# 3x3 convolutions by transformed tiles: from tiles of four by two pixels to tiles of four by four, with the products on column halves of the array

## The chip, the cores and the metric

The kernel runs on one core of a Trainium2 chip. The metric is device time in microseconds (us). Before the change two runs took 2594.91 and 2595.62 us, with a median of 2595.26 us. Engines have short names below: PE is TensorE (PEld its weight loads), DVE is VectorE, ACT is ScalarE, POOL is GpSimd, and SP is the engine that starts most transfers.

## The reference, cut to what matters

The input x is (8, 512, 32, 32) in float32: eight images of 512 channels. The program is two residual layers, and the first one holds the convolutions that are changed.

```python
cbs = silu(bn(conv2d(x, w)))                 # w is 1x1 or 3x3
t = cbs(gn(x), cv1_w)                        # 1x1, 512 -> 512
ys = [t[:, :256], t[:, 256:]]
for i in range(2):
    z = cbs(ys[-1], m_cv1_w[i], pad=1)       # 3x3, 256 -> 256
    z = bot_attention(z, m_qkv_w[i], ...)    # 4 heads, 1024 positions
    ys.append(ys[-1] + cbs(z, m_cv2_w[i]))   # 1x1, 256 -> 256
y = x + cbs(concat(ys), cv2_w)               # 1x1, 1024 -> 512
out = y + L1(gn(y))                          # depthwise 3x3, prune, 1x1, prune
```

So there are 2 x 8 = 16 convolutions of 3x3 in all, called l=0 and l=1 of each batch.

## The kernel before, in words

**Order of the work.** The eight batches are unrolled one after the other. Every piece of work is a small function that is registered under a short name with `add` (line 307). Four strings, FIRST (45), HEAD (64), TAIL (80) and LAST (87), list these names in the order in which the pieces are issued, and `go` (310) issues them. The wrapper `InOrder` (95) keeps that order on each engine, so no scheduler moves anything. Batch 0 runs FIRST; every later batch runs HEAD and then TAIL or LAST. HEAD holds the new batch's 1x1 convolution `cv1`, its first 3x3 convolution, attention and second 3x3 convolution, and beside them what remains of the previous batch's second layer: the depthwise taps `t` on DVE (594) and the pointwise products.

**One convolution** (`conv3`, 725). The input lies in `yp`, split by column phase: pixel column 4t + r is stored under r, so a tile of four columns is read without strides. An output tile is four pixels wide and two high; 6 x 4 = 24 products for each of 128 tiles replace the nine taps. The pieces are:
- `d`: `along_rows` (746) makes `vtmp` and `v`, `across_rows` (774) makes the operands in `kr`, `vt` and `qy`, one for each j = 0, 1, 2. All of this is on DVE, but for four border strips on ACT.
- `P`: `products` (791), six pieces (j by output half m) of 16 matmuls of 128x128 weights by 128 columns. Each takes one tile of 1.05 MB from the weight ring.
- `Rc` and `R`: `rows_back` (810). ACT copies a quarter of the product bank ps_c to `c`; DVE adds the rest from the bank, four instructions of 256 elements.
- `B` and `E`: `along_back` (833) and `ends` (853), on DVE. `Ez`: `close` (858), the silu on ACT that makes half m of `z`.

**Around it.** `c`/`ca` and `y`/`ya` are the halves of `cv1` with their activations (684); `k`, `ka`/`kd`, `v`/`va` and `q`/`qa` are the key, value and query products (`qkv`, 890) into the banks ps_qk and ps_v, which need `z`; `m`, `ma`, `mr` are the 1x1 convolution after the attention (`cv2m`, 1077), with `mr` the residual that writes the next `yp`. The last convolution of batches 1 to 6 (`quartered`, 1243) leaves partial sums `kept` from the banks ps_q on DVE, which run beside the second 3x3 convolution.

**Weights.** In batch 0 `transform_weights` (322) makes the 24 transformed planes of each layer's weights on DVE and ACT and stores them in device memory (`store`, 349), six tiles of 1.05 MB for each layer. From then on every convolution loads them through a ring of five buffers (`ring_sources` 388, `ring_load` 413), which also carries the other large weights. Work tiles share a pool of 11 buffers; the product banks are two pairs of PSUM banks (`big_tile`, 162).

The engines' instructions all appear under L105 in the profile, the line of the wrapper, so groups are told apart by their tiles.

Of the kernel before, what the change touches and what calls it, by code (L numbers as in the profile page):

```python
# [27 lines left out]
PITCH = F // 4 + 1  # L28
# [17 lines left out]
    g*6 gm gd gv g gp g gb gm gd ga gv ga c gp fo gb c ta0 ga ta0 ga ta0 ti0 fo ta2 to0*2 c  # L46
    ti0*2 ca ta2*2 c rl ca ta1*3 ti2 ti1 to1 d ti1 d y ya to1 ti1 y ya ti2 to2 d y ti2 d to2 rl
    ya y d*2 ya d P Rc R P d*3 Rc R d*2 P Rc R B P Rc R B*2 P*2 Rc R E Ez B Rc R E Ez k*2 X k dw
    ta0 ka k kp ka ta0*2 v kp ti0 v va ti0 v ti0 q v va ta1 q ta1 qa q*2 qa ta1 s e s e p to0 s
    e p w to0 s e w*2 ti1 s e p ti1*2 p s e p w s to1 s e p w e p w s w to1 ta2 e s e w h p z  # L50
    ta2 s e p ta2 s ti2 e w*2 s e w ti2 to2 ti2 s e w s e to2 w s e w s e w s e rh p w p*5 h z
    s*2 w e*2 n s e w p s p w nr e p w nr*2 s e nc s nr e ns p w s e p w*2 nc s e p w h z s e s
    w s*2 p*2 e w p e*2 p sc p w sc s w e p w s e p w*3 h z n nr*4 ns nc sc Q K m ma sc dp mr
    m*2 ma mr m ma mr ma mr d*4 Q nc K d*3 P d P Rc R d*2 Rc R d*2 P Rc R P*2 Rc B R B P Rc R E
    Ez Rc B*2 R E Ez k X dx k*3 ka*2 kp*2 v*2 q v*2 va*2 cw*3 rk cw q*2 qa q qa s*2 e*2 p s e p
    w s e w s p cw*2 e s e w s e p rk p w s e p*2 s e w s e g*2 w*2 p w h z s e w cw s e p*2
    cw*2 rk s e w*2 s e w s*2 p e rk w p s e g w p g p s*2 e g w g e*2 p w h z p s w e g p w n
    nr s e nr p w g s e s p w nr e s e w p w*2 s nr p e s e w h ns p s e p nc*2 s w e p w s e p
    w s e p w s sc e p s e p w sc w*3 h z n nr*2 Q nr*2 ns z Q sc*2 nc m*2 ma mr ma mr m ma nc m
    ma mr gm mr gd Q gv u A Q x u i A x i gp i*2 Q gb ga*4 Q im id Q iv A Q x ip i*2 ib b bm t*3  # L60
    Q A t x i*2
# [3 lines left out]
    t c*2 t b im id bm c ca iv t ip t l t*2 ib lr b t*3 c bm ca b y d y bm d ya d*2 ya d*3 y P d  # L65
    Rc R d*2 P Rc R d ya P d Rc R B P Rc R P B*2 Rc R E P Ez Rc B R E Ez y k*3 ya k ka X lp ka
    kd*2 t*5 v*2 l t va v*2 va t lr q*2 t*2 lp t q qa s q e qa s e p s t e w t s e w l s*2 p*2 w
    e*2 p w s p e s w t s w t e s e p lr e p w*2 h z s e p w s t w s p s e p e*2 w*2 p s e w s t
    e p s w p s e w e t p*2 w lp t h z s*2 e*2 w s*2 n e p*2 e w*2 s nr s p e w nr e p s e w nr
    s nr t p ns l w e p*2 w lr lp w ot h s e s w p ot w s w s e*2 p*2 e w p s e w s e ot p*2 z  # L70
    sc w nc w*2 h n nc o O nr ok Ok z nr*2 sc nr ns o ou oa O*2 Ou sc Oa m sc nc m*2 ma*2 m ma
    mr ot mr ma mr o nc mr ou d Ou o O d ou Ou o d O ou*2 oa Ou*2 d Oa o O P d*2 Rc d*3 R P d*2
    Rc R d P Rc P R B Rc P B Rc P R B*2 Rc R ou E oa Ou R Oa o O dp E Ez*2 X k v k v ou oa Ou
    fr*2 Oa ka kd f*2 fr*2 f*2 dx va k v*2 k va q*4 ka kd qa*2 s*3 e*2 p e w p s e w s*2 e*2 p*3
    w s*2 g e*2 w*2 s p e w*2 s e w p s*2 h g e g p w s w z p e*2 s w e g*2 s*2 w*2 p e*2 g p*3
    g s w*2 e p s e w h s*2 e*2 p z p w*2 s p e p s n nr*3 w e s g e p w p s w*3 e p s nc e nr s
    ns e nc w s h s p w z w e p s e w s p e*2 p sc s w e p*2 w s sc e p w*3 h n nr*4 ns z
# [3 lines left out]
    Q*2 K r2 nc r0 Q r2 sc Q m r0 sc K m*2 ma nc mr ma m r0*2 ma mr r1*2 mr Q*3 ma mr r2 r1*2 u0  # L81
    r2 a0 u1 gm a1 gd Q x1 u0 r3 gv x0 gp r3*2 u0 Q r3 gb u0*2 Q u0 a0 i a0 ga Q i x0*2 ga Q i
    u0 a0 i im id ga Q iv ip u1 x0 Q u1*2 ib u1 b a1 x1 bm Q ga u1 t a1 i t Q x1 u1 i*2 a1 t i t
    x1
# [3 lines left out]
    Q sc nc*2 m ma m sc m*2 ma rg ma mr*2 ma mr*2 Q*2 A x Q i*2 im id rg iv ip ib b bm Q*2 t A x  # L88
    i*2 Q im id t*3 iv ip t ib t Q t b Q bm t Q*2 t A t l lr x i*2 im t lp id t iv ip t A ib t b
    bm Q t A x t*2 l lr o x i*2 o lp o*2 im t id t o*3 iv ip t*2 o ib b t*3 bm t o*4 t*2 o*4 l t  # L90
    lr lp t*4 l lr lp o*10 oa o*2 oa fr f oa*2 fr f o*3 oa o oa fr oa f oa fr f
# [34 lines left out]
def fast_kernel(  # L126
# [54 lines left out]
    def load(dst, b):  # L181
# [14 lines left out]
    yp = [const_tile([P, 4, 2, F, PITCH], f"yp{l}") for l in range(2)]  # L196
# [9 lines left out]
        [dram.tile([P, 2, 4, 2, P], F32, tag=f"u{l}_{i}", name=f"u{l}") for i in range(6)]  # L206
# [43 lines left out]

    for t in yp:
        nc.gpsimd.memset(t, 0.0)
# [5 lines left out]
    sc12 = const_tile([P, 4], "sc12")  # L258

    def fold_norms():  # L260
# [8 lines left out]
        ab = const_tile([P, 8], "ab")  # L269
        nc.vector.tensor_tensor(ab, v_sb[:, V_AB : V_AB + 8], sc[:, BN4:], ALU.mult)  # L270
        nc.vector.tensor_tensor(bi[:, BN4:], bi[:, BN4:], ab, ALU.add)
        nc.vector.tensor_scalar(sc12, sc[:, BN2 : BN2 + 4], -1.0 / 12.0, None, ALU.mult)
        yield

    dw = v_sb[:, V_DW : V_DW + 9 * KC].rearrange("p (c t) -> p c t", t=9)
# [1599 lines left out]
```

## Time and profile before

| | |
|---|---|
| median of two runs | 2595.26 us |
| span of the profiled execution | 2593.6 us |
| instructions | 36377 |
| PE busy | 2557.7 us (99%) |
| PE weight loads | 1292.0 us (50%) |
| DVE busy | 2054.9 us (79%) |
| ACT busy | 1214.4 us (47%) |
| POOL busy | 129.2 us (5%) |
| moved by DMA | 268.51 MB, 104 GB/s on average |

Times of groups and stages come from the one profiled execution. In a timeline or a list of groups a line gives the engine, the operation, the tile written and the tiles read with partitions x elements, the count, and the idle time before it with what ended it. In a table of windows each engine has its busy time and, in brackets, its number of instructions; the last columns are the granted PE clock as a share of full speed, the share of time that the DMA engines were busy, and GB/s.

### The profile page before, as it was taken

What the parts mean: (1) busy time and instruction counts of PE and PEld (TensorE: products, weight loads), DVE (VectorE), ACT (ScalarE), POOL (GpSimd) and SP (SyncE); (2) the same over time, 40 slices, a digit from 0 to 9 for tenths busy, and PEclk for the clock granted to TensorE, in tenths of its full rate; (3) what the DMA queues carried; (4) which work ended last, traced back from release to release, by engine and by line L of the source; (5) the groups of instructions that cost most, each with busy time, mean ns of one, the idle gap of its engine ahead of it and who ended that gap; (6) DMA issues with size and microseconds to landing.
All of it is one profiled execution on the core that took longest, in us unless ns stands there. A gap on an engine that the chain in (4) does not pass through costs nothing.

```text
span 2593.6 us, 36377 instructions
## 1 busy us (share of the span) xinstructions
PE 2557.7 (99%) x14806; PEld 1292.0 (50%) x14806; DVE 2054.9 (79%) x2954; ACT 1214.4 (47%) x1551; POOL 129.2 (5%) x99
## 2 busy tenths in 40 slices
PE   8999999999999999999999999999999999999997
PEld 5454463634636346463464635545355544645443
DVE  8887588877897877877778778787788877888657
ACT  3635446353463544635445444544445454363534
POOL 1000000000100000000000000000001000010000
PEclk9999999999999999999999999999999999999998
DMA  9445230522305214060140702306122151312300
GB/s 347 157 155 203 66 122 25 167 98 73 113 27 199 66 65 122 17 247 18 65 122 17 248 18 81 105 24 241 33 96 75 61 204 34 130 45 82 122 17 34
DMA packets 83791, 268.51 MB, mean 104 GB/s; under 512 B 7072, under 2 KB 37536, under 8 KB 69408
## 3 DMA queue, kind: packets, MB, share of 16 engines
q1 hardware_dynamic: 76032, 248.01, 27.2%
q0 software_dynamic: 4032, 14.68, 3.1%
q10 hardware_dynamic: 3552, 3.41, 0.4%
q8 instruction: 118, 1.93, 0.3%
q14 instruction: 57, 0.47, 0.1%
HBM read 212.34 MB, written 36.96 MB: 96 GB/s over the span
## 4 chain that ended last, share of the span: by engine, by line
PE 95%; DVE 3%; ACT 1%; issue 0%; DMA 0%; SPq 0%; DVEq 0%; ACTq 0%
PE ps_av L105 16%; PE ps_s L105 16%; PE ps_c L105 13%; PE ps_cv L105 12%; PE ps_qk L105 8%; PE ps_cv2q L105 8%; PE ps_q L105 7%; PE ps_v L105 4%; PE ps_y L105 4%; PE ps_m L105 4%; PE ps_dn L105 1%; ACT qy L105 1%; DVE sum L105 1%; DVE ht L105 1%; PE ps_pw L105 0%
## 5 line engine op out<-in xcount | busy, mean ns | idle before, releaser
L105 ACT ACTIVATE e<-ps_s 128x1024 f32<-128x1024 f32 x512 | 509.7, 1023 | 286.8 <-PE ps_s L105 265.6
L105 PE MATMUL ps_s<-qy,kr 64*64 64x512 f32 x4096 | 513.7, 592 | 1.4
L105 DVE TENSOR_TENSOR sum<-sum,e 128x1024 f32<-128x1024 f32 x384 | 475.2, 1238 | 39.2 <-ACT e L105 19.9
L105 PE MATMUL ps_av<-e,vt 64*64 64x512 f32 x4096 | 506.2, 590 | 0.0
L105 DVE SCALAR_TENSOR_TENSOR ht<-xn,v_sb,ht 128x961 f32<-128x961 f32 (+1 forms) x256 | 317.3, 1247 | 8.6 <-ACT ht L105 5.0
L105 PEld LDWEIGHTS ps_s<-qy,kr 64*64 64x64 f32 x4096 | 160.5, 132 | 289.0 <-issue 191.1
L105 PEld LDWEIGHTS ps_av<-e,vt 64*64 64x64 f32 x4096 | 165.4, 133 | 277.4 <-issue 266.0
L105 PE MATMUL ps_qk<-z,wring 128*128 128x512 f32 x512 | 231.1, 596 | 2.0 <-ACT z L105 1.3
L105 DVE TENSOR_TENSOR sum<-e 128x1024 f32<-128x1024 f32 x64 | 78.1, 1220 | 164.0 <-ACT e L105 162.6
L105 ACT COPY c<-ps_c 128x256 f32<-128x256 f32 x96 | 35.6, 371 | 259.4 <-PE ps_c L105 259.3
L105 PEld LDWEIGHTS ps_qk<-z,wring 128*128 128x128 f32 x512 | 95.6, 190 | 115.7 <-issue 101.5
L105 DVE RECIPROCAL r<-ps_dn 128x128 f32<-128x128 f32 x128 | 113.7, 925 | 11.2 <-PE ps_dn L105 9.0
L105 PE MATMUL ps_c<-vt,wring 128*128 128x128 f32 x1024 | 119.4, 276 | 2.3 <-DVE v L105 1.3
L105 PEld LDWEIGHTS ps_c<-kr,wring 128*128 128x128 f32 x1024 | 116.8, 192 | 8.0 <-issue 6.1
L105 PEld LDWEIGHTS ps_c<-vt,wring 128*128 128x128 f32 x1024 | 116.2, 192 | 4.3 <-ACT c L105 2.3
L105 PE MATMUL ps_c<-qy,wring 128*128 128x128 f32 x1024 | 117.0, 275 | 0.0
L105 PE MATMUL ps_c<-kr,wring 128*128 128x128 f32 x1024 | 117.0, 275 | 0.0
L105 PE MATMUL ps_cv<-pt,w_sb 128*128 128x512 f32 x256 | 116.7, 607 | 0.0
L105 PE MATMUL ps_v<-wring,z 128*128 128x256 f32 x512 | 115.9, 379 | 0.7 <-DVE kr L105 0.7
L105 PEld LDWEIGHTS ps_c<-qy,wring 128*128 128x128 f32 x1024 | 115.6, 192 | 0.0
L105 PE MATMUL ps_m<-z,wm_sb 128*128 128x512 f32 x256 | 112.5, 592 | 0.0
L105 PE MATMUL ps_y<-pt,w_sb 128*128 128x512 f32 x256 | 112.3, 592 | 0.0
(178 smaller groups left out, 3255.5 us busy)
## 6 DMA issues: line engine op xcount, KB each, us to landing
wring<-u SPq DMA_DIRECT2D x96, 1024.0 KB, 4.8
pt<-in_x SPq DMA_DIRECT2D x32, 512.0 KB, 9.4
rw<-r SPq DMA_DIRECT2D x64, 256.0 KB, 3.4
xt<-in_x SPq DMA_DIRECT2D x32, 512.0 KB, 7.5
out<-xt SPq DMA_DIRECT2D x32, 512.0 KB, 8.0
kr<-r POOLq DMA_DIRECT2D x28, 512.0 KB, 6.6
wring<-q SPq DMA_DIRECT2D x14, 896.0 KB, 4.6
wring<-in_wqkv SPq DMA_DIRECT2D x16, 768.0 KB, 4.4
```

The source lines that it names most:

```text
L105: made = method(*args, **kwargs)
```

## The change

The output tiles become four by four: 6 x 6 = 36 products for each of 64 tiles. Pixels in `yp` and in the first layer's tensors are stored by row phase as well as by column phase. The transform along the rows' direction comes first (`by_rows`, into a new buffer `vrows`), then `along_rows` makes the operands for each j. `products` has nine pieces for each convolution instead of six; each goes over four units (m, row), and its 32 matmuls take 128 rows by 64 columns of weights, on the two column halves of the array (o = 0 and 64) in turn, with 64 moving columns. `rows_copy` copies the whole of each product bank (512 and 256 elements) to SBUF on ACT, and `rows_back` works from these copies with small DVE instructions. The weight transform makes four inner rows from three where it made two, and each layer has nine ring tiles instead of six. The activations in `cv1` and `quartered`, the positions and the last residual are cut into two or four instructions, since the phases now nest deeper. The key products are always in the order of z's halves. The four order strings are written anew for these pieces. Of `conv3` only new lines are shown below; those they replace stand in the kernel above.

```diff
...
@@ -25,7 +25,7 @@
 V_BN, V_AB, V_DW, V_RW, V_RH = 0, 96, 104, 140, 268
 V_N = 396
 LIMIT = 1e20
-PITCH = F // 4 + 1
+ROWS = F // 4 * (F // 4 + 1)
 NWORK = 11
 NRING = 5
...
-    yp = [const_tile([P, 4, 2, F, PITCH], f"yp{l}") for l in range(2)]
+    yp = [const_tile([P, 2, 4, 4, ROWS], f"yp{l}") for l in range(2)]
...
     u_dram = [
-        [dram.tile([P, 2, 4, 2, P], F32, tag=f"u{l}_{i}", name=f"u{l}") for i in range(6)]
+        [dram.tile([P, 4, 2, 2, P], F32, tag=f"u{l}_{i}", name=f"u{l}") for i in range(9)]
         for l in range(2)
     ]
...
+    vrows = const_tile([P, 6, 8, HD], "vrows")
...
+    def half_of(l, m, n):
+        if l == 0:
+            t = yp[0][:, m, :, 2 * n : 2 * n + 2, F // 4 :]
+        else:
+            t = yp[1][:, n].rearrange("p q (r k) x -> p q r k x", k=2)[:, :, :, m, F // 4 :]
+        return t.rearrange("p q r x -> p r q x")
...
-                tt(t, planes[j, 0], planes[j, 2], ALU.add)
-            elif step == 1:
+                if step == 0:
+                    tt(t, first, last, ALU.add)
+                else:
+                    stt(t, last, 4.0, first, ALU.mult, ALU.add)
+            elif step in (1, 4):
                 u = work_tile("ucomp")
-                tt(u, box[j], planes[j, 1], ALU.add)
-                store(j, 1, u)
+                if step == 1:
+                    tt(u, box[j], mid, ALU.add)
+                else:
+                    stt(u, mid, 2.0, box[j], ALU.mult, ALU.add)
+                store(j, step // 3 * 2 + 1, u)
             else:
                 t = box.pop(j)
-                tt(t, t, planes.pop((j, 1)), ALU.subtract)
-                store(j, 2, t)
-        def outer_rows(j, c, dy):
+                if step == 2:
...
-                for i in range(6):
+                for i in range(9):
                     yield u_dram[l][i].rearrange("p a b c d -> p (a b c d)"), 2048
...
         def first_end(m):
-            act(inner(yp[0], m - 2), by_phase(flat(open_.pop(m))), AF.Silu, BN0 + m)
+            out = yp[0][:, m - 2, :, :, F // 4 :].rearrange("p q r (i t) -> p r q i t", t=F // 4)
+            src = by_phase(flat(open_.pop(m)))
+            for q in range(4):
+                act(out[:, :, q], src[:, :, q], AF.Silu, BN0 + m)
...
         def half_end(m, n):
-            dst = phases(y0[:, m, :])[:, :, n * 16 : n * 16 + 16]
-            act(dst, by_phase(banks.pop((m, n))), AF.Silu, BN0 + m)
+            dst = phases(y0[:, m, :])[:, :, :, n * 4 : n * 4 + 4]
+            src = by_phase(banks.pop((m, n)))
+            for r in range(4):
+                act(dst[:, r], src[:, r], AF.Silu, BN0 + m)
...
         comps = [t.rearrange("p a b -> p (a b)") for t in (kr, vt, qy)]
...
+        temps, banks, copies = {}, {}, {}
+        slot = {5: 0, 0: 1, 1: 2, 2: 3, 3: 4, 4: 5}
+        slots = vrows if l else vrows.rearrange("p s (r k) x -> p s r k x", k=2)
+        def like(t, o):
+            return t.rearrange("p (g x) -> p g x", x=HD) if len(o.shape) == 3 else t
+        def by_rows(n, step):
+            y = yp[l][:, n]
+            if l == 0:
+                o = [slots[:, slot[k], :, n] for k in range(6)]
+                both = slots[:, :2, :, n]
+            else:
+                o = [flat(vrows[:, slot[k], 4 * n : 4 * n + 4]) for k in range(6)]
+                both = vrows[:, :2, 4 * n : 4 * n + 4]
+            if step == 0:
+                temps["ab"] = work_tile("vtmp")[:, :512]
+                temps["four"] = work_tile("vtmp")
+            ab, four = temps["ab"], temps["four"]
+            own = y[:, :, :, n8:].rearrange("p q g x -> p (q g) x")
+            low, high = own[:, :8], own[:, 8:]
+            a, b = (like(ab[:, i * 256 : (i + 1) * 256], o[0]) for i in range(2))
+            d = [like(four[:, i * 256 : (i + 1) * 256], o[0]) for i in range(4)]
+            parts = four.rearrange("p (s x) -> p s x", s=4)
+            if step == 0:
+                stt(ab.rearrange("p (g x) -> p g x", x=HD), low, -4.0, high, ALU.mult, ALU.add)
+            elif step == 1:
+                tt(o[1], b, a, ALU.add)
+            elif step == 2:
+                tt(o[2], b, a, ALU.subtract)
+            elif step == 3:
+                out = parts[:, 0:4:2].rearrange("p s (g x) -> p s g x", x=HD)
+                tt(out, y[:, 2:, :, n8:], y[:, :2, :, n8:], ALU.subtract)
+            elif step == 4:
+                near, far = (
+                    bass.AP(
+                        y.tensor,
+                        y.offset + at,
+                        [y.ap[0], [4 * ROWS - n8, 2], [ROWS, 4], [1, HD]],
+                    )
+                    for at in (2 * n8, 8 * ROWS + n8)
+                )
+                out = parts[:, 1:4:2].rearrange("p s (g x) -> p s g x", x=HD)
+                tt(out, near, far, ALU.subtract)
+            elif step == 5:
+                stt(o[3], d[0], 2.0, d[2], ALU.mult, ALU.add)
+            elif step == 6:
+                stt(o[4], d[0], -2.0, d[2], ALU.mult, ALU.add)
+            else:
+                i0, i1 = (
+                    i.rearrange("p s (g x) -> p s g x", x=HD) for i in (parts[:, 0:4:3], parts[:, 1:3])
+                )
+                stt(both, i0, -4.0, i1, ALU.mult, ALU.add)
+        n6 = 6 * P
+        zf = z.rearrange("p a b -> p (a b)")[:, : 2 * n6]
+        low, high = (zf.rearrange("p (s r x) -> p r s x", r=2, x=P)[:, i] for i in range(2))
         def along_rows(j, step):
+            p, q = (
+                comps[j][:, i * n6 : (i + 1) * n6].rearrange("p (s x) -> p s x", x=P)
+                for i in range(2)
+            )
+            if step == 0 and j < 2:
+                v = vrows.rearrange("p s (h g) x -> p h s (g x)", h=2)
+                out = zf.rearrange("p (s x) -> p s x", s=6)
+                if j == 0:
+                    stt(out, v[:, 0], -4.0, v[:, 1], ALU.mult, ALU.add)
+                else:
+                    tt(out, v[:, 1], v[:, 0], ALU.subtract)
+            elif step == 0:
+                v = vrows.rearrange("p s (r k) (i t) -> p r s (k i) t", r=4, t=n8)
+                a, b = (t.rearrange("p s (q t) -> p s q t", t=n8) for t in (p, q))
+                e = n8 - 1
+                tt(a[:, :, :, 1:], v[:, 1, :, :, 1:], v[:, 3, :, :, :e], ALU.subtract)
+                nc.scalar.copy(a[:, :, :, 0], v[:, 1, :, :, 0])
+                tt(b[:, :, :, :e], v[:, 0, :, :, 1:], v[:, 2, :, :, :e], ALU.subtract)
+                nc.scalar.mul(b[:, :, :, e], v[:, 2, :, :, e], -1.0)
+            elif j == 0:
+                tt(p if step == 1 else q, high, low, ALU.add if step == 1 else ALU.subtract)
+            elif j == 1:
+                s = 2.0 if step == 1 else -2.0
+                stt(p if step == 1 else q, low, s, high, ALU.mult, ALU.add)
+            elif step == 1:
+                stt(p, p, -4.0, high, ALU.mult, ALU.add)
+            else:
+                stt(q, low, -4.0, q, ALU.mult, ALU.add)
+        place = {1: 0, 3: 1, 2: 2, 4: 3, 0: 4, 5: 5}
+        def products(j, part):
+            u = ring.pop(0).rearrange("p (x i k o) -> p x i k o", x=4, i=2, k=2)
+            for x in range(4):
+                m, row = UNITS[4 * part + x]
+                if (j, m) not in banks:
+                    banks[j, m] = big_tile("ps_c3")
+                ps = flat(banks[j, m])
+                for i in range(2):
+                    at = place[row] * P + i * HD
+                    for k in range(2):
+                        from_ = ((i * 6 + slot[row]) * 2 + k) * HD
+                        for o in (0, HD):
+                            nc.tensor.matmul(
+                                ps[o : o + HD, at : at + HD],
+                                u[:, x, i, k, o : o + HD],
+                                comps[j][:, from_ : from_ + HD],
+                                start=(k == 0),
+                                stop=(k == 1),
+                            )
+            ring_load()
+        inner_planes, outer_planes, ys = {}, {}, {}
+        def rows_copy(j, m, part):
+            if (j, m) not in copies:
+                copies[j, m] = work_tile("c1")
+            c = slice(0, 512) if part == 0 else slice(512, 768)
+            nc.scalar.copy(copies[j, m][:, c], flat(banks[j, m])[:, c])
+        def rows_back(j, m, step):
             if step == 0:
...
+                temps["sd"] = work_tile("c2")
                 if j == 0:
...
+                    inner_planes[m] = work_tile("mid")
+                if j == 2:
+                    outer_planes[m] = copies[j, m]
+            c, sd = copies[j, m], temps["sd"]
+            if step == 0:
+                tt(sd[:, :256], c[:, :256], c[:, 256:512], ALU.add)
+                tt(sd[:, 256:512], c[:, :256], c[:, 256:512], ALU.subtract)
                 return
...
             dst = outer_planes[m][:, :512] if j == 2 else inner_planes[m][:, j * 512 : j * 512 + 512]
...
+            o = dst.rearrange("p (q y x) -> p q y x", q=2, x=HD)
+            s1, s2, d1, d2 = (
+                sd[:, i * P : (i + 1) * P].rearrange("p (q x) -> p q x", x=HD) for i in range(4)
+            )
+            stt(o[:, :, 0], s2, -0.25, s1, ALU.mult, ALU.add)
+            stt(o[:, :, 3], d2, -2.0, d1, ALU.mult, ALU.add)
+            stt(o[:, :, 1], d2, -0.5, d1, ALU.mult, ALU.add)
+            tt(o[:, :, 2], s1, s2, ALU.subtract)
+            e = o[:, :, 0:4:3]
+            outer = c[:, 512:768].rearrange("p (y q x) -> p q y x", y=2, q=2)
+            tt(e, e, outer, ALU.subtract)
...
-        for j in range(3):
-            add("d", *[lambda j=j, i=i: along_rows(j, i) for i in range(2)])
-            add("d", *[lambda j=j, i=i: across_rows(j, i) for i in range(2)])
-        add("P", *[lambda j=j, m=m: products(j, m) for j, m in jm])
-        add("Rc", *[lambda j=j, m=m: rows_back(j, m, 0) for j, m in jm])
-        add("R", *[lambda j=j, m=m: rows_back(j, m, 1) for j, m in jm])
+        add("dr", *[lambda n=n, i=i: by_rows(n, i) for n in range(2) for i in range(8)])
+        add("d", *[lambda j=j, i=i: along_rows(j, i) for j in range(3) for i in range(3)])
+        add("P", *[lambda j=j, i=i: products(j, i) for j in range(3) for i in range(3)])
+        parts = ((0, 0), (0, 1), (1, 1), (1, 0))
+        add("Rc", *[lambda j=j, m=m, i=i: rows_copy(j, m, i) for j in range(3) for m, i in parts])
+        add("R", *[lambda j=j, m=m, i=i: rows_back(j, m, i) for j, m in jm for i in range(2)])
...
         order = [(k, m) for m in (2, 3) for k in range(2)]
-        add("k", *[lambda m=m, k=k: products(m, k) for k, m in (sorted(order) if by_input else order)])
+        add("k", *[lambda m=m, k=k: products(m, k) for k, m in (sorted(order))])
...
         def residual(n, m):
-            r = slice(2 * n, 2 * n + 2)
-            dst = inner(yp[1], m) if l == 0 else phases(qy[:, m, :])
-            nc.vector.tensor_tensor(dst[:, r], phases(ts[n, m]), inner(yp[l], m)[:, r], ALU.add)
+            dst = half_of(1, m, n) if l == 0 else by_rq(qy[:, m, n * 512 : (n + 1) * 512])
+            nc.vector.tensor_tensor(dst, by_rq(ts[n, m]), half_of(l, m, n), ALU.add)
         for name, piece in (("m", products), ("ma", norm), ("mr", residual)):
...
     def to_rows(m, n, t):
-        o = xt[m].rearrange("p (h t r) -> p h t r", t=F // 4, r=4)[:, :, :, 2 * n : 2 * n + 2]
-        i = t.rearrange("p (r h t) -> p h t r", h=F, t=F // 4)
-        nc.vector.tensor_tensor(o, i, o, ALU.add)
+        o = xt[m].rearrange("p (i q t r) -> p i q t r", q=4, t=F // 4, r=4)
+        o = o[..., 2 * n : 2 * n + 2]
+        i = t.rearrange("p (r q i t) -> p i q t r", q=4, i=F // 4, t=F // 4)
+        for r in range(2):
+            nc.vector.tensor_tensor(o[..., r], i[..., r], o[..., r], ALU.add)
     def combine_weights(p):
```

## The prediction

> **What bounds the kernel now.** I read the page first: busy time by engine, the slices, the chain, the costliest groups.
>
> ```profile
> PE 2557.7 (99%) x14806; PEld 1292.0 (50%) x14806; DVE 2054.9 (79%) x2954; ACT 1214.4 (47%) x1551; POOL 129.2 (5%) x99
> ...
> PE   8999999999999999999999999999999999999997
> ...
> DVE  8887588877897877877778778787788877888657
> ...
> PE 95%; DVE 3%; ACT 1%; issue 0%; DMA 0%; SPq 0%; DVEq 0%; ACTq 0%
> ...
> L105 PE MATMUL ps_c<-kr,wring 128*128 128x128 f32 x1024 | 117.0, 275 | 0.0
> ```
>
> TensorE (PE) is never idle and is the chain; the three ps_c groups (the 3x3 products, 3072 records) are 353 us of it. VectorE (DVE) at 79% looks free, but that is a mean. So next the windows of the stages that hold a convolution: first layer (cv1 to qkv), second layer (cv2m to qkv), both of batch 2. Columns: length, then busy of PE, PEld, DVE, ACT, POOL.
>
> ```profile
> 639.15:688.50 49.35, 49.35 (x262) 34.05 (x260) 47.70 (x90) 18.92 (x29) 1.56 (x2) 1.00 0.38 132
> 776.54:820.83 44.29, 44.24 (x246) 31.26 (x244) 39.63 (x79) 12.82 (x27) 0.00 (x0) 1.00 0.36 124
> ```
>
> DVE is at 97% of the first stage. Of the second, its timeline from the last residual to the last correction:
>
> ```profile
> 784.42 0.69 DVE L105 TENSOR_TENSOR yp<-m,yp 128x512 f32<-128x512 f32 x1 [0.97 <-ACT m L105]
> 785.32 0.69 DVE L105 TENSOR_TENSOR kept<-kept,ps_q 128x512 f32<-128x512 f32 x1 [0.21 <-PE ps_q L105]
> ...
> 788.93 1.28 DVE L105 TENSOR_TENSOR kept<-kept,ps_q 128x512 f32<-128x512 f32 x2
> 790.13 1.28 DVE L105 TENSOR_TENSOR kr<-v 128x512 f32<-128x512 f32 x2
> ...
> 810.10 1.09 DVE L105 SCALAR_TENSOR_TENSOR y<-sd 128x256 f32<-128x256 f32 x3
> 811.10 0.41 DVE L105 TENSOR_TENSOR y<-sd 128x256 f32<-128x256 f32 x1
> ...
> 820.18 0.69 DVE L105 TENSOR_TENSOR y<-y,mid 128x512 f32<-128x512 f32 x1
> ```
>
> After 785.32 DVE has no gap to 820.87. ACT then makes the second half of z (ends 822.14 in its timeline), and PE's first values product, which needs all of z, starts at 822.64. DVE is late by half a microsecond of becoming the bound. In the first stage z is complete at 689.51 and its first user could start at 690.2: 0.7 us. So the convolution stages have two bounds, and a change that eases PE and loads DVE is judged by DVE.
>
> **What the skill says.** "TensorEngine Tiling (Array Packing)", Key Properties: different tiles can load weights and multiply in parallel. The trace agrees for 64x64 quadrants: score matmuls start 6 to 7 ns apart in fours, 429 ns per four. Column halves of 64 with all 128 rows do not occur. The same page, Instruction Overhead: about 60 cycles per matmul, so a moving size under that gains nothing; 64 is just above it, and no run shows it. "TensorE: Matmul & The Clock Gate", LDWEIGHTS: the load scales with columns; the trace has 192 ns at 128 columns, 132 at 64, 108 at 32. The same page, Part 1: about 3.4 us of idle halves the PE clock; the trace agrees near the end:
>
> ```profile
> 2566.03 16.82 PE L105 MATMUL ps_pw<-ht,wring 128*128 128x512 f32 x32 [4.74 <-DVE wring L105]
> ```
> ```profile
> 2565.00:2570.00 5.00, 3.98 (x5) 1.85 (x6) 4.86 (x7) 0.00 (x0) 0.00 (x0) 0.50 0.00 0
> ```
>
> A 4.7 us wait, then clock 0.50 (column after POOL).
>
> **PE's part.** Before, a convolution has 96 matmuls of two records; records start 112 ns apart: 96 x 2 x 0.1117 = 21.4 us (about 7.3 for each j in its timeline). After: 288 matmuls of two records, in 144 pairs on two halves, moving size 64. If halves run together, a pair takes for each of its two passes half of 112 plus a few ns, 58: 144 x 2 x 0.058 = 16.7 us, say 16.8. Saving 4.6 us, 16 times: 74 us. Bounds: nothing less than the arithmetic (75% of before, 16 us); if halves take turns, or issue (never shown denser than one record per 107 ns) binds, 33.6 us. I take 16.8.
>
> **DVE's part.** From the rows above, start to start: 0.333 us at 256 elements (three in 1.00), 0.60 at 512 (two in 1.20), so 0.07 + 1.04 ns per element; 128: 0.20, 768: 0.87, 1536: 1.67 (extrapolated). An instruction that needs the one just before adds 0.12 (v from vtmp: 1.33 for two, not 1.20).
> Before, per convolution: input transform 18 x 0.60 + 6 x 0.57 = 14.2; rows_back 24 x 0.333 = 8.0; along_back and ends 6.3. Sum 28.5.
> After: by_rows 8 x 0.60 + 8 x 0.335 = 7.5; along_rows for j=0 and j=1 one of 1536 and two of 768 each (1.67 + 1.74 = 3.4), for j=2 two of 672 and two of 768 (1.54 + 1.74 = 3.3), 10.1; rows_back, six times three of 256 and four of 128: 10.8; along_back and ends 6.3. Sum 34.7. So +6.2, and about ten more direct dependences, +1.2.
>
> **Second-layer stage** (batches 1 to 7). Summing the ordered DVE list from the last residual to the last correction with these prices: 34.6 us before (measured 35.6), 39.5 after, since one partial sum moves out; with the dependences +6.1. Less the 0.5 of slack: +5.6 us for the values products and all behind them. On the way: the first product needs all of by_rows and j=0 of along_rows, 11.5 + 1 us after 785.1, while PE has five ps_q groups (8.6 us) from 783.4. It waits some 6 us, and the clock may halve; PE's 20 us of products then still fit in DVE's remaining 29. PE's saving goes into waits.
>
> **First-layer stage** (1 to 7). From the last quadrant sum before it (640.01) the list grows 43.6 to 48.8, one tap being done earlier; +1.2 gives 6.4, less 1.1 of DVE idle and 0.3 of packing: z at 694.5. The key products are reordered so that two need only z's first half: the stage's four end at 694.5 + 3.43 = 697.9 against 695.4. +2.6.
>
> **Batch 0.** Its weight transform forms four rows inside (1, 2, 3, 4) where it formed two: three more 1024-wide instructions per j, 9 x 1.14 = 10.3 us per layer. For the first layer this lies ahead of the products: DVE's list from 23.0 us on is 34.5 + 2 us to the first product (59.6, before 43.7), then 26 to the end: z at 87, before 71.1. +16. DMA alone says +18: three more tiles of 1.05 MB stored and three loaded, 6.3 MB at the 350 GB/s seen there. They run side by side; I take 16, plus 2 for the second layer's 10 us, mostly in attention, where DVE has 7.6 us of idle in 57.7. Second stage of batch 0: +5.6.
>
> **At nothing:** the copies out of the product banks, now all of each bank (512 in 0.48 us and 256 in 0.27, start to start, where one of 256 was made): +2.9 us of ACT per convolution, ACT being at 29 to 38% there. They free a bank while PE fills the other, 1.87 us per part; without that cover each of six would show 0.5 us; split activations and residuals; three ring tiles more per convolution, 1.05 MB at 4.8 us, hidden while DVE sets a pace of about 3 us per tile. Without that cover, at 1.9 us per tile, the later ones would come 1 to 3 us late. SP issues them in its order; in batch 0 they stand behind the stores of the same j, which is in the 18 us above.
>
> Sum: 7 x (5.6 + 2.6) + 5.6 + 16 + 2 = 81 us; 2593.6 + 81 = 2674.6. The runs' median is 1.7 above the profiled span (2595.3), so 2676.
>
> **Rivals.**
> DVE bound as summed: 2645 to 2730 (a third less or two thirds more than the 81 us). 0.64.
> Hidden in part: DVE idles 13.6 us between 600.5 and 639.15, just ahead of the first stage. If taps move there so that DVE no longer ends it, PE's 4.6 us show: 7 x (4 - 3) + 24 = 31 us, so about 2626, 2615 to 2645. It decides where the ordered list moves over 5 us; it moves one tap. 0.18.
> Other side: PE stays the only bound, dependences and small instructions cost less, and 74 us come through: 2593.6 - 74 + 18 = 2538, 2540 with the median. It needs DVE's growth under the 0.5 and 0.7 us of slack. 0.04.
> Halves take turns: products 33.6 us, end of stage 4.6 us behind the last: second stage 797.6 + 33.6 + 3.4 + 4.6 = 839 against 822 (+17), first +11, batch 0 +26 and +18, in all 7 x 28 + 44 = 240: 2593.6 + 240 = 2834, say 2835. For it: no column half and no such rate in the trace. Against: ps_dn on 128x32 tiles runs four at once, 7 ns apart. 0.14.
>
> **Numbers.** The range takes in the first two: 2620 to 2740. A measurement tells about 2% from no change (2543 to 2647). Faster 0.04; same 0.18; slower 0.78.
>
> **What would show it.** DVE without gaps in both stages; PE waiting on DVE kr and on ACT z, some 6 us ahead of the second layer's first product; ps_c busy near 270 us; first product near 60 us; DVE busy up by about 120 us. Wrong if ps_c groups stay near 350 us or more, if the small DVE instructions differ from 0.20 and 1.67, or if PE waits on the ring.

## The result, and the profile after

The changed kernel takes 2723.98 us (median of two runs, 2721.36 and 2726.59) against 2595.26 before: a ratio of 1.0497, interval 1.0467 to 1.0528. That is slower by 129 us where 81 us were forecast; 2724 lies inside the range of 2620 to 2740. The profiled execution has a span of 2719.6 us, 126.0 us longer.

The first part of the page:

```profile
span 2719.6 us, 49469 instructions
PE 2541.0 (93%) x20950; PEld 1242.5 (46%) x20950; DVE 2197.2 (81%) x3354; ACT 1302.8 (48%) x1748; POOL 133.2 (5%) x111
...
PE   4898999999999999989999899998999999999997
...
DVE  7987778877988779887788877887788877988657
...
L105 PE MATMUL ps_c<-vt,wring 128*64 128x64 f32 x3072 | 102.3, 223 | 24.0 <-ACT c L105 8.9
```

PE lost its unbroken row of nines. Its busy time fell by 17 us only, and 179 us of the span are now idle on PE. DVE's busy time grew by 142 us. The ps_c groups sum to 320 us (353 before), but a busy figure there holds waits inside a run of matmuls: in the raw records a pair on the two halves starts 7 ns apart and the next pair 51 to 52 ns later, 58.4 ns for a pair and pass, the 58 that was forecast.

What PE waits for (engine, tile, releaser; us in total, times, longest):

```profile
PE ps_c L105 <- DVE kr L105: 46.1, 28, 12.0
PE ps_c L105 <- ACT c L105: 28.4, 48, 0.7
PE ps_c L105 <- issue: 21.5, 23, 6.5
PE pm L105 <- DVE mv L105: 20.3, 10, 8.6
PE ps_y L105 <- ACT y L105: 11.2, 1, 11.2
PE ps_c L105 <- DMA wring<-u: 8.8, 15, 1.7
```

Before, the first three stood at 1.3 (for its `v`), 0.7 and nothing. So PE does wait for DVE ahead of the first product, but three other releasers, ACT's bank copies, the ring, and "issue", hold almost 60 us together.

The two stages of batch 2 again (length; busy of PE, PEld, DVE, ACT, POOL; clock, DMA share, GB/s), from cv1 to the keys and from cv2m to the keys:

```profile
695.22:746.78 51.56, 46.92 (x645) 30.17 (x644) 50.38 (x103) 22.93 (x44) 1.34 (x1) 1.00 0.48 174
835.71:886.11 50.40, 43.97 (x630) 29.17 (x629) 46.50 (x99) 15.81 (x30) 0.00 (x0) 0.93 0.47 175
```

They were 49.35 and 44.29 us. DVE fills 98% and 92% of them. The clock of 0.93 in the second stage is new: in every second layer of batches 1 to 7 it was granted at 0.50 for 3.4 or 6.8 us at the start of the products, ahead of which PE sits idle for 4.0 us, and while it lasts a pair takes 107 ns in place of 58. Before, both windows had 1.00. From the second layer's last residual on, DVE's timeline has three gaps of 0.2 to 0.5 us and ends 5.9 us later, counted from the end of cv2m, than before:

```profile
843.59 0.69 DVE L105 TENSOR_TENSOR yp<-m,yp 128x512 f32<-128x512 f32 x1 [0.37 <-ACT m L105]
...
852.71 1.76 DVE L105 SCALAR_TENSOR_TENSOR z<-vrows 128x1536 f32<-128x1536 f32 x1
854.50 1.83 DVE L105 TENSOR_TENSOR kr<-z 128x768 f32<-128x768 f32 x2
...
885.36 0.69 DVE L105 TENSOR_TENSOR y<-y,c 128x512 f32<-128x512 f32 x1
```

To see where 126 us come from, each batch and layer is measured from the end of one cv2m to the end of the next (PE's ps_m records):

| us | before | after | grew by | forecast |
|---|---|---|---|---|
| batch 0, first layer, with the start | 160.8 | 196.6 | 35.8 | 18 |
| batch 0, second layer | 126.9 | 135.8 | 8.9 | 5.6 |
| first layer, batches 1 to 7 | 1277.2 | 1307.0 | 29.8 | 18.2 |
| second layer, batches 1 to 7 | 933.0 | 984.3 | 51.3 | 39.2 |

### The profile page after: what moved, and what is told of

The parts are those of the page before. It is cut to its first block, busy times and chain, and to the rows that moved or that the text cites. A ratio compares the mean times of both kernels' runs of the same rounds, so it can differ in the third digit from the quotient of the medians.

```text
span 2719.6 us, 49469 instructions
## 1 busy us (share of the span) xinstructions
PE 2541.0 (93%) x20950; PEld 1242.5 (46%) x20950; DVE 2197.2 (81%) x3354; ACT 1302.8 (48%) x1748; POOL 133.2 (5%) x111
## 5 line engine op out<-in xcount | busy, mean ns | idle before, releaser
L105 PE MATMUL ps_qk<-z,wring 128*128 128x512 f32 x512 | 228.7, 595 | 11.6 <-ACT vt L105 7.7
L105 ACT COPY c<-ps_c 128x512 f32<-128x512 f32 x192 | 87.5, 482 | 303.5 <-PE ps_c L105 278.3
L105 PE MATMUL ps_c<-kr,wring 128*64 128x64 f32 x3072 | 116.4, 245 | 58.2 <-DVE kr L105 46.1
L105 PEld LDWEIGHTS ps_c<-kr,wring 128*64 128x64 f32 x3072 | 110.9, 159 | 74.7 <-DVE kr L105 52.3
L105 PE MATMUL ps_c<-vt,wring 128*64 128x64 f32 x3072 | 102.3, 223 | 24.0 <-ACT c L105 8.9
L105 PE MATMUL ps_c<-qy,wring 128*64 128x64 f32 x3072 | 101.2, 223 | 23.1 <-ACT c L105 14.0
L105 PEld LDWEIGHTS ps_c<-vt,wring 128*64 128x64 f32 x3072 | 95.0, 138 | 35.0 <-issue 13.6
L105 PEld LDWEIGHTS ps_c<-qy,wring 128*64 128x64 f32 x3072 | 94.8, 138 | 33.2 <-ACT c L105 17.4
```

Of the source, the lines that this page charges most:

```text
L105: made = method(*args, **kwargs)
```

## The experiments

The theory on record was that DVE's list of instructions sets both convolution stages and the start (A). Its rivals were product pieces held by banks, ring or issue (B, F, H). Each kernel ran once, beside a run of the kernel before (2594.2 to 2594.8 us). The changed kernel's two runs differ by 5 us, and its stages by 1 to 2 us from batch to batch, so differences under some 6 us are read from the table of stages, not from the total.

**More DVE work in the kernel before.**

```diff
...
             pairs[j] = work_tile("v")
+            for i in range(4):
+                tt(more[:, i % 2], more[:, 2], more[:, 2], ALU.add)
```

> The kernel before, with twelve more DVE additions of 512 elements in each 3x3 convolution (four for each j, on a scratch tile that nothing reads, so no result changes): 12 x 0.60 = 7.2 us of DVE, about the 6.2 + 1.2 us that the change adds, and nothing else of the change. Theory A (DVE's list of instructions sets the end of a convolution stage, with 0.5 us of slack in the second layer and about 1.4 in the first): second layer +6.7 us, first +5.8, in all 8 x 6.7 + 7 x 5.8 + 7 = 101 us, so about 2697. Theory B (the loss comes from the new products, their banks and their ring tiles, and DVE's growth is mostly covered): under 20 us, so below 2616.

2698.66 us. Second layers 140.3 (forecast 140.0), first layers of batches 2 to 7 188.4 to 189.9 (forecast 188.7). DVE alone, with no other part of the change, costs as much as was said. The kernel before had no room on DVE.

**Halves one after the other.**

```diff
-                for i in range(2):
+                for o, i in ((0, 0), (0, 1), (HD, 0), (HD, 1)):
...
-                        for o in (0, HD):
+                        if True:
```

> The changed kernel with each unit's eight matmuls reordered: the four of the lower column half first, then the four of the upper, so that neighbours nearly always lie on the same half. Theory A (in the changed kernel the two halves run at once, 58 ns for a pair and pass, and PE has waits in hand): products alone take 288 x 2 x 0.058 = 33.4 us for each convolution, more than the 22 to 27 us from first to last that they take now, so PE ends the stage: about +10 us in the first layer and +12 in the second, 8 x 22 = 176 us, about 2900. Theory C (the halves take turns already, or the queue pairs them whatever their order): no change, 2724.

2762.14 us: neither. At the full clock a record starts 37.8 ns after the one before it on average, in place of 29.7 (waits left out). That is 4.7 us for each convolution, 75 us in all, and 38 of them show. Seven in ten records still start in close pairs, 15 ns apart or less, where nearly all did. Halves overlap although neighbours in the program lie on the same half; taking turns in fours costs a quarter more time, not double.

**Order of the start.**

```diff
-    ... gm gd ta0 c gv gp fo gb ga*2 ta0 c ta0 ...
+    ... gm gd gv gp fo gb ga*2 ta0 c ta0 c ta0 ...
-    ... ca ti2*6 dr*3 to2*2 y ya dr*4 ta1*3 ti1*6 ...
+    ... ca ta1*3 ti2*6 dr*3 to2*2 y ya dr*4 ti1*6 ...
```

> The changed kernel with two moves in the order of batch 0 alone: the second half of the group norm's products goes ahead of the first cv1 products, and the weight planes of j=1 are formed before the transform of j=2 and not after it. Theory A (DVE's list sets the start; it begins its first weight sum 3.8 us later than before since the norm's small product stands behind 5.1 us of cv1 on PE, and idles 4.8 us for ACT's planes): 7 to 9 us less, first product near 61 us, about 2716. Theory D (the stores and loads of the weights set the start): less than 2 us less.

2725.43 us. The first product comes at 65.9 in place of 69.0. DVE's idle time did not go away; it got another releaser. In the changed kernel, then in this one:

```profile
37.70 1.23 DVE L105 TENSOR_TENSOR ucomp<-uplane 128x1024 f32<-128x1024 f32 x1 [4.79 <-ACT uplane L105]
```

```profile
38.16 1.23 DVE L105 TENSOR_TENSOR ucomp<-uplane 128x1024 f32<-128x1024 f32 x1 [1.58 <-DMA u<-uplane]
41.84 2.48 DVE L105 TENSOR_TENSOR ucomp<-ucomp,uplane 128x1024 f32<-128x1024 f32 x2 [2.45 <-DMA u<-uplane]
```

DVE now waits 4.0 us for stores to give work tiles back. The start has both bounds, DVE's list and the stores behind it. Elsewhere nothing was changed, and stages came out between 0.9 us shorter and 2.3 us longer.

**Taps later.** In HEAD, five `t` from the first convolution to just behind its keys.

```diff
-    ... dr*3 t*2 dr ip ... c t ca ... Rc t d t ya ... d t Rc ya ... kd t*5 v
+    ... dr*3 t dr ip ... c ca ... Rc d ya ... d Rc ya ... kd t*10 v
```

> The changed kernel with five depthwise taps (five DVE instructions of about 961 elements, 5 x 1.15 = 5.7 us) of batches 1 to 7 moved from the first-layer convolution to just behind its keys. Nothing else moves. Theory A (DVE's list sets the end of this stage, and attention has room): the fourth key product ends 4 to 5.7 us earlier, 7 x 4.5 = 31 us, about 2692. Theory B (PE's product waits for banks and ring set it): no change. Theory E (DVE has no room in attention): the gain is given back by the next layer's start, no change in all.

2723.95 us. First layers of batches 2 to 7 take 186.9 on average against 187.5, 0.6 us for 5.7 us of DVE taken away, close to theory B. Attention did not take the gain (theory E): from the fourth key product to the end of cv2m it is 88.4 us in both kernels. DVE, lighter, waits for ACT's copies of the product banks instead. So in this stage DVE's list was not the only bound: something as long lies right behind it.

**Products first.** Example from HEAD:

```diff
-    y*2 P Rc t d t ya R d*4 P*2 Rc*2 P R Rc R*2 Rc P Rc ...
+    y*2 P*3 Rc t d t ya R d*4 Rc*3 P*3 R*3 Rc*2 R*2 ...
```

> The changed kernel with the order of FIRST and HEAD altered so that the three product pieces of each j stand together, ahead of ACT's four copies (before, a copy of one part of a bank pair often stood between two pieces that write other parts of the same pair, and PE waited 0.69 us for it, 48 times in all). Theory F (in the first layer PE's own chain of products, waits and banks is as long as DVE's list, so these waits count there; the second layer is DVE's): first to last product 2 us shorter in the first layer, nothing in the second, 8 x 2 = 16 us, about 2708. Theory A alone (DVE sets both): no change, 2724.

2738.83 us, slower, as neither theory said. The waits for the copies are gone, and the others have taken their place:

```profile
PE ps_c L107 <- DVE kr L107: 43.0, 27, 8.9
PE ps_c L107 <- issue: 35.2, 27, 6.5
...
PE ps_c L107 <- DMA wring<-u: 14.7, 27, 1.5
...
PE ps_c L107 <- ACT c L107: 0.3, 1, 0.3
```

First to last product stays at 22.3 us in the first layer (22.7 with the old order), and from there to the end of the fourth key product it takes 12.4 us where it took 10.8, with more of the copies now behind the last product. The waits for the ring and "issue" grew together from 30.3 to 49.9 us. The copies' 0.69 us were not what held the products' pace.

**Two steps on POOL.**

```diff
-                tt(out, near, far, ALU.subtract)
+                nc.gpsimd.tensor_tensor(out, near, far, ALU.subtract)
```

and the same for the step ahead of it.

> The changed kernel with two of the eight steps of by_rows, for each of its two halves, given to POOL (512-element subtractions, 0.60 us each on DVE). DVE loses 4 x 0.60 = 2.4 us in each convolution. Theory A (DVE sets the second layer's stage): 2.4 us less for each second layer, 0.5 to 1 for each first layer, 8 x 2.4 + 7 x 0.7 + 2 = 26 us, about 2698. Theory G (POOL is three times slower for such sizes, 0.9 us for 256 elements in this trace, and delays the first product by more than DVE gains): no gain, or up to 3 us more for each convolution, 2724 to 2770.

2739.39 us: theory G. The first product does come later, by 0.6 us in the second layer and 1.6 in the first, and there is a reason that theory G did not name. POOL and DVE around the residuals of batch 2:

```profile
854.00 1.27 POOL L790 TENSOR_TENSOR vtmp<-yp 128x512 f32<-128x512 f32 x1 [1.23 <-DVE yp L105]
855.23 1.44 POOL L801 TENSOR_TENSOR vtmp<-yp 128x512 f32<-128x512 f32 x1
```

```profile
853.84 0.67 DVE L105 TENSOR_TENSOR kept<-kept,ps_q 128x512 f32<-128x512 f32 x1
854.44 2.51 DVE L105 TENSOR_TENSOR vrows<-vtmp 128x256 f32<-128x256 f32 x2
856.87 1.35 DVE L105 SCALAR_TENSOR_TENSOR vrows<-vtmp 128x256 f32<-128x256 f32 x3
```

The two vrows<-vtmp additions take 2.51 us while POOL runs; without it they take 0.75. A DVE instruction that reads two operands from SBUF stands still under POOL's; the one that reads a PSUM bank (kept) keeps its 0.67. The Trainium skill says this on the page "SBUF — State Buffer", section "SBUF: two separate sides": DVE with two SBUF inputs and POOL share a pair of ports, held by one of them for a whole instruction. The trace agrees, with 1.76 us more for the two. What was taken off DVE was given back as standstill.

**Half of the ring's bytes.**

```diff
-                    yield u_dram[l][i].rearrange("p a b c d -> p (a b c d)"), 2048
+                    yield u_dram[l][i].rearrange("p a b c d -> p (a b c d)")[:, :1024], 1024
...
-                                u[:, x, i, k, o : o + HD],
+                                u[:, x % 2, i, k, o : o + HD],
```

> The changed kernel with only half of each product tile loaded (0.52 MB for each of the nine in place of 1.05), the matmuls using that half twice, and the convolution's scale made smaller so that all values stay finite: the weights of half of the units are left out and replaced by the others. All instructions of PE, DVE and ACT are as they were. Theory H (the ring's loads, 350 to 410 GB/s without a pause during the products, hold PE back): first to last product 1 to 3 us shorter in each layer, 16 x 2 = 32 us, about 2692, and the same stage repeats within 0.3 us from batch to batch. Theory A: under 6 us in all, most of it in batch 0.

2705.31 us, 19 us less (16 between the profiled executions) with every instruction of the engines in place. That lies between the two forecasts. First to last product 21.3 us (22.7) in the first layer and 25.3 (26.8) in the second; second layers all lie between 139.0 and 139.4 (140.3 to 141.0). PE's waits:

```profile
PE ps_c L105 <- DVE kr L105: 48.8, 28, 14.9
PE ps_c L105 <- ACT c L105: 28.4, 48, 0.7
...
PE ps_c L105 <- issue: 9.4, 5, 6.9
```

No wait for the ring is left in this list, and of 23 "issue" gaps 5 remain. So half of the ring's bytes is worth 16 to 19 us, and most "issue" gaps go with it: 19 of the 23 fall in the middle of a tile, where no operand changes, and of those one is left. An instruction queue moves 16 KB about every 5.5 us there, and in the changed kernel each of the 19 gaps ends 2.2 to 3.0 us after such a packet starts. That PE then waits for its own instructions, late on busy DMA engines, fits this and was not tried by itself.

**Without the added weight sums.**

```diff
-                    stt(t, last, 4.0, first, ALU.mult, ALU.add)
...
-                    stt(u, mid, 2.0, box[j], ALU.mult, ALU.add)
...
-                    stt(t, mid, -2.0, t, ALU.mult, ALU.add)
```

> The changed kernel without the three DVE instructions of 1024 elements that form the two added inner rows for each j of the weights: the second inner row is stored in their place, so as many stores and loads remain, and the convolution's scale is made smaller so that all values stay finite. DVE loses 9 x 1.2 = 11 us ahead of batch 0's first product and 11 us in its first attention. Theory A (DVE's list sets batch 0's start and adds to its first attention): first product near 58 us (now 69), the first attention some 5 us shorter, about 2708. Theory D (the stores, 6.3 MB for the nine tiles at once beside the loads, set the start): first product at most 4 us earlier, about 2720.

2719.88 us. The first product comes at 61.2 in place of 69.0, 7.8 us earlier for 11 us of DVE; batch 0's first layer takes 187.3 in place of 196.6. The start came 25.3 us later than before the change, so these sums are under a third of that. The result lies between the two theories. The total moves by 4 only, as other stages came out up to 2 us longer.

**Without the partial sums.**

```diff
         def plus(o, x, name):
-            nc.vector.tensor_tensor(banks[name] if o is None else kept[o], kept[x], banks[name], ALU.add)
+            return
```

> The changed kernel without the seven partial sums of each pair of channel blocks in the pointwise convolution of the second network layer (DVE instructions of 512 elements, reading a ps_q bank; nine of them stand between the last residual and the end of the second 3x3 convolution, in batches 1 to 7). DVE loses 9 x 0.60 = 5.4 us there. Theory A (DVE's list sets the second layer's stage): the fourth key product ends 4.5 to 5.4 us earlier in each of seven second layers, nothing in the first, 7 x 5 = 35 us, about 2689. Theory H (the ring's loads set it): under 1.5 us each, 2714 or more.

2718.28 us. Second layers take 139.5 on average against 140.6: 1.1 us, not 5, though DVE's busy time up to the keys fell from 41.8 to 36.6 us in batch 2. DVE's list is not the only bound of this stage. PE, then DVE, in that stage of batch 2:

```profile
868.23 2.09 PE L105 MATMUL ps_c<-vt,wring 128*64 128x64 f32 x64 [0.46 <-DMA wring<-u]
870.57 2.08 PE L105 MATMUL ps_c<-vt,wring 128*64 128x64 f32 x64 [0.26 <-DMA wring<-u]
873.05 2.09 PE L105 MATMUL ps_c<-vt,wring 128*64 128x64 f32 x64 [0.40 <-DMA wring<-u]
...
882.82 2.08 PE L105 MATMUL ps_c<-qy,wring 128*64 128x64 f32 x64 [0.98 <-DMA wring<-u]
```

```profile
872.39 0.76 DVE L105 TENSOR_TENSOR c<-c 128x256 f32<-128x256 f32 x2 [3.17 <-ACT c L105]
...
885.56 0.76 DVE L105 TENSOR_TENSOR c<-c 128x256 f32<-128x256 f32 x2 [1.57 <-ACT c L105]
```

The time taken off DVE comes back as a DVE wait for ACT's copy, which waits for the product, which waits for its ring tile. Tiles start some 2.4 us apart here, where the products alone need 1.87.

**Full columns.**

```diff
-                        for o in (0, HD):
+                        if True:
...
-                                ps[o : o + HD, at : at + HD],
-                                u[:, x, i, k, o : o + HD],
+                                ps[:, at : at + HD],
+                                u[:, x, i, k, :],
```

> The changed kernel with each pair of matmuls on the two column halves made one matmul of 128 columns by 64 moving: 144 matmuls of two passes for each convolution in place of 288, the same arithmetic. Theory I (the weight load of 128 columns, 192 ns in the kernel before against a pace of 112 ns, cannot follow 64 moving columns): a pass keeps to about 112 ns, products 144 x 2 x 0.112 = 32 us for each convolution against 17 to 18 now without waits, +10 us or more for each, 16 x 10 = 160, about 2880. Theory J (a pass takes half of 112 whichever way the columns are cut): products 16.5 us, no change, 2724, or some us less since half as many instructions are fetched.

3261.09 us, worse than either theory. A pass takes 112 ns at 64 moving columns, as it does at 128 in the kernel before, and for much of the time 213. The windows inside a second layer's products (the column after POOL is the clock):

```profile
1047.00:1065.00 18.00, 17.96 (x84) 17.96 (x85) 12.53 (x20) 0.86 (x2) 0.00 (x0) 0.50 0.32 115
1065.00:1080.00 15.00, 15.00 (x103) 13.32 (x103) 5.18 (x17) 2.40 (x5) 0.00 (x0) 0.83 0.47 158
1080.00:1095.00 15.00, 13.82 (x111) 12.59 (x111) 9.60 (x27) 4.22 (x8) 0.00 (x0) 1.00 0.68 237
```

The 112 ns are no floor for every instruction, since two matmuls on column halves start 7 ns apart. At a clock of 1.00 the pass is bound by something that does not shrink with the moving columns. The Trainium skill, "TensorE: Matmul & The Clock Gate", section "LDWEIGHTS (loading the stationary operand)", gives a load as its columns over 1.2 in ns: an estimate of 107 for 128 columns, near the measured pass of 112, and of 53 for 64, near the 51 to 52 between the pairs of the changed kernel. The trace's own load records last longer, 192 ns at 128 columns and 138 at 64, but they overlap one another and start 112 ns apart. So the pass came out as theory I said; its cause, the load, fits and is not shown by itself. The theory lacked the clock, granted at 0.50 although PE shows busy throughout, which doubles the pass. The same page, Part 1, ties the clock to how busy PE is; no run here shows what it counts as busy. The column halves carry the change: with whole columns it costs 666 us, not 129.

**A lighter DVE; a lighter DVE and half the ring.** The first joins four runs above: products first, taps later, without the added weight sums, without the partial sums. The second adds half of the ring's bytes.

> The changed kernel with DVE made lighter around each convolution and the product pieces of each j together: without the partial sums (as in the run without them), five taps later, without the added weight sums of batch 0, smaller scale. It leaves out those sums and planes 3 and 4 of the weights. Ring loads are whole. Theory H (with DVE out of the way, the ring of five tiles at 350 to 410 GB/s sets the products' pace): first to last product stays at 21 us or more in both layers, about 2670. Theory K (PE's gain appears as soon as DVE is lighter): first to last product 17 to 18.5 us, about 2620.

> As the run with a lighter DVE, and with half of each product tile loaded as in the run with half the ring's bytes. Theory H: first to last product falls to 17 to 19 us, and against the run with a lighter DVE alone the whole falls by 2 to 4 us for each convolution, 16 x 3 = 48 us, about 2620. Theory K: no difference between the two.

2713.61 and 2672.93 us. With DVE lighter alone, first to last product takes 21.9 and 26.9 us (22.7 and 26.8 in the changed kernel), and layers 187.6 and 140.2 us; most of the 10 us gained are batch 0's (187.7 us in its first layer in place of 196.6). With half the ring as well it takes 20.2 and 23.0 us, and layers 185.9 and 136.3. That is theory H's kind of answer, 41 us between the two runs for its 48, though the products stay above its 17 to 19. The same half gave 19 in the changed kernel. That the lighter DVE alone makes this difference is not shown: both runs also have the products first, an order that by itself raised the waits for the ring and "issue" from 30.3 to 49.9 us. They are 56.5 with DVE lighter, and 13.8 with half the ring as well. No run halves the ring under that order with DVE's whole list.

In the last run the clock shows too. From the first to the last product of the second layer, batch 4 and then batch 5 (columns as above):

```profile
1485.88:1507.70 21.82, 21.40 (x585) 18.59 (x586) 21.04 (x52) 5.65 (x12) 0.00 (x0) 1.00 0.58 183
1806.18:1830.40 24.22, 24.04 (x585) 21.18 (x585) 21.12 (x52) 5.65 (x12) 0.00 (x0) 0.87 0.53 167
```

The second layers of batches 4 and 7 have no stretch at 0.50 and take 134.9 us both; the other five have 3.4 to 6.2 us of it in their products and take 136.4 to 137.4. In the changed kernel, where all seven have it, no such order is seen.

## Why the prediction was right, and where it was short

The range held, partly because it was wide: the profiled executions differ by 125.8 us up to the last cv2m where 81 were summed. Of the 44.8 us that are missing, 21.1 lie in batch 0, 11.6 in the first layers and 12.1 in the second layers, and none of them was in the sum. Of the signs that were named, DVE nearly without gaps and PE's waits for kr came true. The wait ahead of the second layer's first product was 4.0 us, not 6, the first product came at 69.0, not 60, and ps_c took 320 us, neither 270 nor 350. One sign of being wrong came true as well: PE waits on the ring, 8.8 us in 15 waits.

**PE's part** was right: 58.4 ns for a pair and pass, for 58. The rival of halves in turn falls with it. The gain went, as said, into waits.

**DVE's prices** were right: 0.202 us at 128 elements, 0.87 at 768, and DVE busy up by 142 for 120. That the kernel before had no slack there was shown by loading it.

**Second layer**: z was forecast 5.6 us late and came 6.0 late (from 39.2 to 45.2 us after cv2m, to the first values product). The rest of the 7.3 us lies behind it: the keys and values come in a new order, and PE waits 1.1 us for a bank that ACT still copies from (ps_qk, for vt). This wait was left out.

**First layer**: z was forecast 55.35 us after the stage's start and is complete at 55.3, the fourth key product at 58.75 and 58.92. So the 2.6 us of this stage hold. The 1.7 us more lie in the stage ahead: a group norm product waits 1.3 us for DVE, where the last residual, now cut in two, takes 1.08 us for 512 elements in place of 0.61. The prediction put that split at nothing. Batch 1, which has no such stage ahead of it, grew by 2.5 us; the split was not undone by itself.

**The step of the mechanism that failed is "at nothing: three ring tiles more".** It took them as hidden while DVE sets a pace of 3 us per tile. Halving all nine tiles takes off 16 to 19 us as the kernel stands, and 41 with DVE lighter and the products first. The halving removes 4.7 MB from each convolution and the three tiles are 3.1 MB, so their own price was not measured. The mechanism chosen, DVE as the bound of both stages, is therefore half of the answer: loading DVE lengthens the stages, but relieving it by 5.4 and 5.7 us shortens them by 1.1 and 0.6 only. The forecasts of z fit because both chains end within about a microsecond of each other; that PE's chain, whose waits were not summed, is as long as DVE's was luck. When both are eased the second layer takes 136.3 us, against 133.3 in the kernel before. Where the clock was not halved it takes 134.9, and its first values product then comes 0.5 us earlier after cv2m than in the kernel before, so the rest lies behind z. The prediction allowed for the clock to halve and took it as covered by DVE's list.

**Batch 0** was mis-sized: 44.7 us for 23.6. Of the 25.3 us by which the first product is late, the nine added sums are 7.8. DVE begins its first weight sum 3.8 us later, since a group norm product now stands behind 5.1 us of cv1 on PE's queue, and idles 4.8 us for ACT's planes; moving both gave 3.1, with new waits for the stores. The forecast of 59.6 and these two waits add up to 68.2, near the 69.0 seen. They were not read from the order, though it shows the first. (For z in this layer the prediction's 59.6 and 26 add up to 85.6, not 87; and a third less than 81 us gives 2649, not 2645.) The first attention grew by 7.1 us where 2 were forecast; without the added sums it is 2.4 us shorter.

## What to carry to other kernels

When two chains of equal length end a stage, loading either one makes it longer and relieving either one alone does little. A test of a bound must relieve it, and look at what the engine then waits for. And a saving on PE that brings more weight bytes per microsecond of products must be priced against the ring at the new pace, not at the pace that another engine happens to keep: here 1.05 MB at the 350 to 410 GB/s seen are 2.6 to 3.0 us a tile, an estimate, where the products alone need 1.87.

## What the runs showed of the hardware that was not expected

- Matmuls with 128 weight columns keep to 112 ns a pass at 64 moving columns as at 128; two matmuls of 64 columns on the two halves take 58.4 for the pair.
- While the clock was granted at 0.50, the same pair took 107 ns, and the full-column pass 213.
- In that full-column form the clock was granted at 0.50 for stretches of 18 us and more with PE busy all the time (17.96 of 18.00 us).
- Two DVE additions of 256 elements, each of two SBUF operands, went from 0.75 us to 2.51 while POOL ran 512-element subtractions; one with a PSUM operand did not change (0.67).
- POOL takes 1.5 us on average for such a subtraction of 512 elements, DVE 0.60.
